# Graph network layer: blocks pick their rows in quarters of 256 edges on 32 partitions each

## The chip, the cores and the metric

The kernel runs on one core of one Trainium2 chip. The time is the device time of one execution in microseconds; it is told as the median of several runs. A profile is one more execution, recorded by the hardware profiler.

## The reference

There are N = 12500 nodes with 64 features and E = 212500 edges, sorted by their destination `dst`. An edge has a source, a destination and one weight. D = 64, H = 128.

```python
h = relu(layernorm(x))                                   # [N, 64]
edge_in = concat([h[src], h[dst], edge_weight1], axis=1)   # [E, 129]
e = silu(edge_in @ eW1 + eb1)                            # [E, 128]
e = silu(e @ eW2 + eb2)
agg = segment_sum(e, src, N)                             # [N, 128]
out = x + silu(concat([h, agg], axis=1) @ nW1 + nb1) @ nW2 + nb2
```

So rows are picked by `dst`, which is sorted, and summed by `src`, which is not.

## The kernel before

**Tables.** The first product is split by its inputs: `ta` holds h times the first 64 rows of eW1 for every node, `tb` h times the next 64. `tb0` is an early copy of the first 2048 rows of `tb`, used by blocks 0 to 29 (`EARLY`).

**Sending.** Edges are taken in blocks of 1024 (`BLK`), two blocks a pair, 104 pairs, 208 blocks. Since `dst` is sorted, 512 neighbouring edges (`HALF`) need only a short stretch of rows of `tb`. For each pair, SP loads a window `win` of four stretches of 58 rows (`WL`), which begin 25 rows (`STEP`) apart; two stretches lie on partitions 0 and up and two on partitions 64 and up (`HB`). Behind each stretch stand two constant rows, the eW1 row of the edge weight (`w1d`) and the bias (`eb1b`), put there once at the start by small POOL DMAs (L219) into three window tiles. `destinations()` works out each edge's row within its stretch and writes it to `dests`; `load_rows` broadcasts these rows to `bc`; `pick` (L368, L370) compares them with the partition's number, which gives a selecting matrix of 128 partitions by 512 columns for each block; the edges' weights go into its weight rows by a DMA (`weights`). The product `qp` (L406) multiplies `pick` and `win`: four f32 matmuls of 128 x 256 per block, each of which the trace records as two passes. ACT copies the result to `qs` (L417), adds the edge's local node number (L428), and POOL scatters 128 rows at a time (L435, eight indirect DMAs per block) into `q`, a table in DRAM that is sorted into buckets of the source node. `count` works out with DVE and two small PE products (`full`, L333 and L374) which row of its bucket each edge gets.

**Summing.** `q` is read back by batches: eleven levels of ranks times 25 groups of four buckets (`fetch`, `qt`, L486). Each of 450 steps handles four tiles of 128 edges: `lr` (L511) and `oneT` (L516) and `one` (L544) make one-hot matrices of the source, `pt` (L525, L531) adds the rows of `ta`, ACT applies silu (L535), `p` (L563) is the second product, ACT again (L567), and `seg` (L577) sums by node into `aggT` (L588). The last level is followed by the node network (`nodes`), in which `z` takes two products: L239 on 128 partitions and L242 on 64 partitions for each of two halves.

**Order.** PE, DVE, ACT and SP run their instructions in the order in which the program writes them (`manual_schedule`); POOL's order is that of the program too. The order of a step is the list `turn`, with gaps (`None`) at which pieces of `send_all` (block s is sent and block s+1 counted), of the feed (tables, checks) and of the node network are put in; a level's blocks are spread over the level before it by `marks`. Before the loop a head runs: constants, the norm of the first nodes (`x0`), `destinations()`, `sources()`, then the first tables and blocks. In the head POOL issues its DMAs and memsets one after the other:

```python
    for win in wins:
        nc.vector.memset(win, 0.0)
        for a in range(2):
            for i, row in enumerate((w1d, eb1b)):
                at = a * HB + WL + i
                for g in range(2):
                    nc.gpsimd.dma_start(win[at : at + 1, g, a, :], row[:1, :])
```

Of the kernel before, what the change touches and what calls it, by code (L numbers as in the profile page):

```python
# [28 lines left out]
F32 = mybir.dt.float32  # L29
F16 = mybir.dt.float16  # L30
BF16 = mybir.dt.bfloat16
I32 = mybir.dt.int32
# [6 lines left out]
P = 128  # L39
L = 125  # L40
WL = 58
STEP = 25
SPAN = 3 * STEP + WL
FEW = 12
HB = 64
BLK = 1024
HALF = BLK // 2
TB = BLK // P
PAIR = 2 * BLK
G = 4  # L50
# [21 lines left out]
def tile_gnn(ctx: ExitStack, tc: tile.TileContext, x, src, dst, ew, eW1, eb1, eW2, eb2, nW1, nb1, nW2, nb2, out):  # L72
# [10 lines left out]
    assert LEVELS[-1][1] == -(-E // BLK) and PAD < BLK and PAD % FEW == 0 and (-PAD) % HALF >= FEW  # L83
# [83 lines left out]
    nc.vector.tensor_scalar(plus, part, HB - 0.5, None, op0=OP.is_gt)  # L167
    nc.vector.scalar_tensor_tensor(same, plus, -float(HB), part, op0=OP.mult, op1=OP.add)
# [19 lines left out]
    dests = dram.tile([NP, 2, 2, HALF], BF16, name="dests")  # L188

    tb0 = dram.tile([P * NE, H], F32, name="tb0")  # L190
# [22 lines left out]
    for win in wins:  # L213
        nc.vector.memset(win, 0.0)
        for a in range(2):
            for i, row in enumerate((w1d, eb1b)):
                at = a * HB + WL + i
                for g in range(2):
                    nc.gpsimd.dma_start(win[at : at + 1, g, a, :], row[:1, :])  # L219
# [42 lines left out]
    with ExitStack() as work:  # L262
# [17 lines left out]
        def load_rows(s):  # L280

            if s < nblocks:
                p, g = s // 2, s % 2
                if g == 0:
                    bc = ld.tile([P, 2, HALF], BF16, name="bc")
                    lists[p] = [bc, None]
                bc, _ = lists[p]
                if g == 0 or p == 0:
                    m = 1 if p == 0 else 2
                    r = dests[p, 0, g]  # L290
                    of = bass.AP(tensor=r.tensor, offset=r.offset, ap=[[BLK, 2], [0, HB], [1, m * HALF]])
                    nc.sync.dma_start(bc[:, g : g + m].rearrange("p g e -> p (g e)"), of)
                blk[s] = [bc[:, g]]

        def load(s):

            if s < nblocks:
                p, g = s // 2, s % 2
                win = wins[p % NW]
                table, end = (tb0, NE * P) if s < EARLY else (tb, NB * P)  # L300
                assert s < EARLY or len(done_b) == NB // G
                if g == 0:
                    at = nc.sync.value_load(base_i[:, p : p + 1], min_val=0, max_val=end - SPAN)
                    for a in range(2):
                        rows = table[bass.ds(at, SPAN), :]
                        of = [[H, WL], [2 * STEP * H, 2], [1, H]]
                        of = bass.AP(tensor=rows.tensor, offset=rows.offset + a * STEP * H, ap=of)
                        nc.sync.dma_start(win[a * HB : a * HB + WL, :, a, :], of)
                    lists[p][1] = ld.tile([P, 2, HALF], F32, name="pick")
                blk[s] += [win[:, g], lists[p][1][:, g]]  # L310
            load_rows(s + 1)

        def weights(s):

            if s < nblocks:
                p, g = s // 2, s % 2
                pick = lists[p][1][:, g]
                e0 = s * BLK
                m = 1 if p == 0 or e0 + 2 * BLK > E else 2
                if m == 2 or e0 + BLK <= E:  # L320
                    of = bass.AP(tensor=ew.tensor, offset=ew.offset + e0, ap=[[HALF, 2], [BLK, m], [1, HALF]])
                    nc.sync.dma_start(lists[p][1][WL::HB, g : g + m, :], of)
                else:
                    for a in range(2):
                        m = min(HALF, E - e0 - a * HALF)
                        if m > 0:
                            of = bass.AP(tensor=ew.tensor, offset=ew.offset + e0 + a * HALF, ap=[[m, 1], [1, m]])
                            nc.sync.dma_start(pick[a * HB + WL : a * HB + WL + 1, :m], of)
# [65 lines left out]
        def send(s):  # L394
# [8 lines left out]
            two = [2 if G + t < nt else 1 for t in range(min(G, nt))]  # L403
            qps = [mm.tile([P, 2, 2, H], F32, name="qp", tag="mm") for _ in range(2)]
            for t, k in enumerate(two):
                nc.tensor.matmul(  # L406
                    qps[t // 2][:, t % 2, :k], pick[:, t * P : (t + 1) * P], win[:, :k], start=True, stop=True
                )
            parts = []
            for i, qp in enumerate(qps):  # L410
                qs = qsp.tile([P, 2, 2, W], F32, name="qs")
                mine = [(t, k) for t, k in enumerate(two) if t // 2 == i]
                same = [(slice(0, 2), 2)] if mine == [(2 * i, 2), (2 * i + 1, 2)] else [
                    (slice(t % 2, t % 2 + 1), k) for t, k in mine
                ]
                for ts, k in same:
                    nc.scalar.copy(qs[:, ts, :k, :H], qp[:, ts, :k, :])  # L417
                parts.append((i, same, qs))
            for i, same, qs in parts:
# [5 lines left out]
                places = locE[:, g * TB : (g + 1) * TB, p].rearrange("p (a i t) -> p i t a", a=2, i=2)  # L425
# [3 lines left out]
                for a in range(2):  # L429
                    for t in range(2 * i, 2 * i + 2):  # L430
                        j = a * G + t
                        if j >= nt:
# [5 lines left out]
                            in_=qs[:k, t % 2, a, :],  # L438
# [191 lines left out]
        def first_rows(g):  # L630

            hr = turned(x0, g)
            yield
            got = fp.tile([P, G, H], F32, name="got")
            product(1, hr, mm, "mm", got)
            yield
            nc.scalar.dma_start(tb0.rearrange("(p j) f -> p j f", j=NE)[:, g : g + G, :], got)
            yield
# [42 lines left out]
        def destinations():  # L681

            nc.scalar.copy(f, dstR)
            lim = lp.tile([NP, 1], F32, name="lim")
            nc.vector.tensor_scalar(lim, part[:NP], EARLY / 2 - 0.5, float((NB - NE) * P), op0=OP.is_gt, op1=OP.mult)
            nc.vector.tensor_scalar(lim, lim, float(NE * P - SPAN), None, op0=OP.add)
            yield
            nc.vector.tensor_scalar(lo[:, 0:1], fv[:, 0, 0:1], lim, None, op0=OP.min)
            for h in range(1, 4):
                nc.vector.tensor_scalar(lo[:, h : h + 1], lo[:, 0:1], float(h * STEP), None, op0=OP.add)  # L690
            for g in range(2):
                nc.vector.tensor_tensor(
                    rowsD[:, :, g, :],
                    fv[:, 2 * g : 2 * g + 2, :],
                    lo[:, 2 * g : 2 * g + 2, None].to_broadcast([NP, 2, HALF]),
                    op=OP.subtract,
                )
            nc.sync.dma_start(dests, rowsD)
            yield
            lot = mm.tile([1, NP], F32, name="lot", tag="mm")  # L700
            nc.tensor.transpose(lot, lo[:, 0:1], ident[:NP, :NP])
# [43 lines left out]
        def checks():  # L745

            ends = lp.tile([NP, 2, 4], F32, name="ends")
# [33 lines left out]
        with tc.tile_pool(name="lists", bufs=1, side="right") as lp:  # L781
# [5 lines left out]
            fv = f.rearrange("p (g e) -> p g e", e=HALF)  # L787
            lo = lp.tile([NP, 4], F32, name="lo")
            rowsD = lp.tile([NP, 2, 2, HALF], BF16, name="rowsD")
# [227 lines left out]
```

## Time and profile before

| | |
|---|---|
| median of 9 runs | 3138.19 us (3122.5 to 3166.21) |
| profiled execution: time | 3132.66 us |
| its span | 3130.4 us |
| mean granted TensorE clock | 0.875 |
| busy: PE / PE weight loads / DVE / ACT / POOL | 76 / 67 / 62 / 35 / 56% of the span |
| instructions | 45060 |
| moved by DMA | 446.69 MB, 143 GB/s in the mean |

A row of a group of instructions gives its line, engine, operation, what it writes and reads, its count, its busy time in us (overlaps counted once), the mean duration of one in ns, and the idle time of its engine just before it with what ended it. PE stands for the matmuls, PEld for the weight loads, which run beside them; SPq and POOLq are the sequencers that issue DMAs. "Clock" is the share of the full TensorE clock that the throttle granted. In a timeline a row has its start, its length, and what was run, with a count where several instructions are merged; a bracket holds the idle time before it.

### The profile page before, as it was taken

How to read it: one execution, taken by the hardware profiler on the slowest of the kernel's cores; microseconds unless marked ns; L12 is line 12 of the kernel's file. 1: busy time of each engine (PE TensorE's matmuls, PEld its weight loads, DVE VectorE, ACT ScalarE, POOL GpSimd, SP SyncE). 2: the span in 40 equal slices, each digit the busy share in tenths (PEclk: the TensorE clock that was granted, in tenths of full speed). 3: DMA queues.
4: the chain of work that ended last, by engine and by line, in shares of the span. 5: the costliest groups of instructions: out<-in, count | busy, mean ns of one | idle time of the engine just before them, and what ended most of it. 6: DMA issues, size and time to landing. Idle time of an engine off the chain costs nothing.

```text
span 3130.4 us, 45060 instructions
## 1 busy us (share of the span) xinstructions
PE 2391.0 (76%) x16009; PEld 2099.6 (67%) x16009; DVE 1955.8 (62%) x2946; ACT 1099.4 (35%) x2409; POOL 1752.6 (56%) x1739
## 2 busy tenths in 40 slices
PE   2665476566687788878887778778778888888998
PEld 1443465555577677767776667667677777788897
DVE  6665365566576666666766667666657767775443
ACT  2431222222233333333333334333334334344443
POOL 3656666666665566665665565656566666653000
PEclk9665688777788989889898899899999999999999
DMA  3543345454555555443443344334434444555441
GB/s 85 182 150 115 105 147 158 155 161 158 157 183 168 182 182 185 160 153 123 137 138 120 124 136 133 125 123 134 132 120 140 136 134 131 162 169 177 136 136 58
DMA packets 217115, 446.69 MB, mean 143 GB/s; under 512 B 41443, under 2 KB 83412, under 8 KB 216677
## 3 DMA queue, kind: packets, MB, share of 16 engines
q1 hardware_dynamic: 141897, 276.38, 27.8%
q0 software_dynamic: 54400, 123.05, 11.5%
q10 hardware_dynamic: 20586, 44.30, 4.8%
q8 instruction: 130, 2.13, 0.3%
q14 instruction: 102, 0.84, 0.1%
HBM read 257.70 MB, written 185.85 MB: 142 GB/s over the span
## 4 chain that ended last, share of the span: by engine, by line
PE 31%; DVE 10%; another core or an unknown queue 5%; issue 4%; DMA 1%; ACT 1%; POOL 1%; DVEq 0%; SPq 0%; ACTq 0%; POOLq 0%
PE p L563 7%; PE seg L577 6%; PE pt L531 6%; PE qp L406 5%; PE pt L525 3%; DVE oneT L516 2%; PE lr L511 2%; DVE one L544 1%; DVE rank L390 1%; DVE oh L340 1%; DVE mine L388 1%; DVE aggT L588 1%; POOL q L435 1%; DMA q<-qs,to 1%
## 5 line engine op out<-in xcount | busy, mean ns | idle before, releaser
L435 POOL DMA_INDIRECT q<-qs,to x1661 | 1709.7, 1029 | 1129.0 <-ACT qs L428 566.9
L535 ACT ACTIVATE e<-pt 128x512 f32<-128x512 f32 x450 | 270.2, 600 | 1110.2 <-remote 358.5
L577 PE MATMUL seg<-one,e 128*128 128x125 f32 x3600 | 528.6, 291 | 145.5 <-DVE aggT L588 82.3
L516 DVE TENSOR_SCALAR oneT<-lr,part 125x512 f32<-125x512 f32 x450 | 336.0, 747 | 447.9 <-remote 180.1
L563 PE MATMUL p<-w,e 128*128 128x128 f32 x3600 | 527.7, 289 | 93.4 <-issue 44.9
L577 PEld LDWEIGHTS seg<-one,e 128*128 128x128 f32 x3600 | 479.4, 204 | 173.5 <-issue 149.5
L563 PEld LDWEIGHTS p<-w,e 128*128 128x128 f32 x3600 | 491.0, 202 | 148.0 <-issue 59.9
L406 PEld LDWEIGHTS qp<-win,pick 128*128 128x128 f32 x1664 | 361.6, 229 | 307.0 <-issue 219.8
L531 PE MATMUL pt<-oneT,a 125*128 125x256 f32 (+1 forms) x2200 | 514.4, 361 | 44.0 <-issue 36.2
L406 PE MATMUL qp<-win,pick 128*128 128x256 f32 x1664 | 512.5, 458 | 23.0 <-issue 15.5
L417 ACT COPY qs<-qp 128x512 f32<-128x512 f32 x418 | 236.5, 585 | 586.0 <-PE qp L406 165.4
L531 PEld LDWEIGHTS pt<-oneT,a 125*128 125x128 f32 x2200 | 362.6, 204 | 81.3 <-issue 50.5
L588 DVE TENSOR_TENSOR aggT<-aggT,seg 128x500 f32<-128x500 f32 x250 | 167.7, 671 | 348.5 <-remote 111.0
L567 ACT ACTIVATE e<-p 128x512 f32<-128x512 f32 x450 | 270.6, 601 | 170.9 <-PE p L563 45.1
L525 PE MATMUL pt<-ident,qt 128*128 128x128 f32 x1800 | 298.5, 288 | 41.3 <-issue 27.8
L348 DVE TENSOR_REDUCE each<-oh 128x100 bf16<-128x800 bf16 x208 | 315.1, 1515 | 7.2
L544 DVE TENSOR_TENSOR one<-nodes,qt 128x500 f32<-128x500 f32 x450 | 302.6, 672 | 0.5 <-PE seg L577 0.5
L557 ACT COPY p<-b2f 128x512 f32<-128x512 f32 x450 | 269.0, 598 | 0.0
L525 PEld LDWEIGHTS pt<-ident,qt 128*128 128x128 f32 x1800 | 207.8, 149 | 82.4 <-issue 46.7
L388 DVE TENSOR_TENSOR mine<-oh,full 128x800 f32<-128x800 bf16 x208 | 203.9, 980 | 77.7 <-remote 35.1
L511 PE MATMUL lr<-identb,qt 128*125 128x128 bf16 x1800 | 191.2, 228 | 49.6 <-issue 30.1
L511 PEld LDWEIGHTS <-qt 128*125 128x125 bf16 x1800 | 172.4, 144 | 68.1 <-issue 56.0
(135 smaller groups left out, 1395.9 us busy)
## 6 DMA issues: line engine op xcount, KB each, us to landing
qt<-q SPq DMA_DIRECT2D x175, 576.0 KB
a<-ta SPq DMA_DIRECT2D x275, 256.0 KB
qt<-q SPq DMA_DIRECT2D x100, 288.0 KB
q<-qs,to POOLq DMA_INDIRECT x1661
bc<-dests SPq DMA_DIRECT2D x103, 256.0 KB
q<-zeros ACTq DMA_DIRECT2D x20, 1080.0 KB
q<-zeros ACTq DMA_DIRECT2D x10, 1440.0 KB
win<-tb SPq DMA_DIRECT2D x208, 58.0 KB
```

Of the source, the lines that this page charges most:

```text
L348: nc.vector.tensor_reduce(each, oh.rearrange("p t b -> p b t"), AX.X, OP.add)
L406: nc.tensor.matmul(qps[t // 2][:, t % 2, :k], pick[:, t * P : (t + 1) * P], win[:, :k], start=True, stop=True)
L435: ins = nc.gpsimd.indirect_dma_start(out=q[:], out_offset=bass.IndirectOffsetOnAxis(ap=to[:k, j : j + 1], axis=0), in_=qs[:k, t % 2, a, :] ...
L511: nc.tensor.matmul(lr[:L, t, :], loc[:, at : at + 1].to_broadcast([P, L]), identb, start=True, stop=True)
L516: nc.vector.tensor_scalar(oneT, st[k].pop("lr")[:L], part1[:L, :], None, op0=OP.is_equal)
L525: nc.tensor.matmul(pt[:, t, :], qt[:, j, :H], ident, is_transpose=True, start=t == 0, stop=False, skip_group_check=True)
L531: nc.tensor.matmul(pt[:, cols, :], a[:L, b, :], oneT[:, cols, :], start=False, stop=True, skip_group_check=True)
L535: nc.scalar.activation(e1, pt, AF.Silu)
L544: nc.vector.tensor_tensor(one.rearrange("p (b j) l -> p b j l", j=n), nodes1[:, None, None, :].to_broadcast(wide), loc[:, tiles[0][1] : ti ...
L563: nc.tensor.matmul(p2[:, t, :], e1[:, t, :], w2, start=False, stop=t == G - 1, skip_group_check=True)
L567: nc.scalar.activation(e2, p2, AF.Silu)
L577: nc.tensor.matmul(item[2][:, b, :], e2[:, t, :], one[:, t, :], start=j < G, stop=j >= G * (n - 1))
```

## The change

A block's 1024 edges are taken in four quarters of 256 edges (`QR`) instead of two halves of 512. Each quarter has a stretch of 30 rows (`WL`), 15 rows (`STEP`) from the next, eight stretches for a pair, on partitions 0, 32, 64 and 96. The constant rows stand at rows 30 and 31 of each 32 partitions, so there are 48 of the small POOL DMAs instead of 24. `bc`, `pick` and `rowsD` have 256 columns a block instead of 512. A window is loaded by four DMAs instead of two. A matmul of `qp` reads 64 partitions (two quarters), 128 columns of `pick` and up to 256 columns of `win` (a quarter's rows stand in one half of the columns and zeros in the other); the four matmuls of a block take the lower and the upper 64 partitions in turn, and the two halves write into different PSUM tiles. The start of a window is the lowest start that any of its eight quarters asks for, found with a subtraction and a minimum over `steps15`, which POOL makes with an iota; it may lie up to 16 rows (`FRONT`) ahead of the table, for which `tb0` gets 16 rows of zeros in front. The last quarter of the last pair holds only filling; its rows are moved by 20 (`far`). In the programs' order PE, ACT and POOL's scatters keep their places in the loop; SP has 208 more window DMAs with their address instructions; in the head, the iota of `steps15` is POOL's last instruction before the scatters, behind the small DMAs and the memsets of `xs`, and DVE's copy of it stands right before the memset of `srcR` (L790) and the first norm (L604).

```diff
-WL = 58
-STEP = 25
-SPAN = 3 * STEP + WL
+WL = 30
+STEP = 15
+SPAN = 7 * STEP + WL
+FRONT = 16
...
-HB = 64
+NQR = 4
...
-HALF = BLK // 2
+QR = BLK // NQR
...
-    tb0 = dram.tile([P * NE, H], F32, name="tb0")
+    tb0 = dram.tile([FRONT + P * NE, H], F32, name="tb0")
+    nc.gpsimd.dma_start(tb0[:FRONT], zeros[:FRONT, :H])
...
-        for a in range(2):
+        for a in range(NQR):
             for i, row in enumerate((w1d, eb1b)):
-                at = a * HB + WL + i
+                at = a * 32 + WL + i
                 for g in range(2):
-                    nc.gpsimd.dma_start(win[at : at + 1, g, a, :], row[:1, :])
+                    nc.gpsimd.dma_start(win[at : at + 1, g, a % 2, :], row[:1, :])
...
-                    bc = ld.tile([P, 2, HALF], BF16, name="bc")
+                    bc = ld.tile([P, 2, QR], BF16, name="bc")
...
-                    of = bass.AP(tensor=r.tensor, offset=r.offset, ap=[[BLK, 2], [0, HB], [1, m * HALF]])
+                    of = bass.AP(tensor=r.tensor, offset=r.offset, ap=[[2 * QR, NQR], [0, 32], [1, m * QR]])
...
-                    for a in range(2):
-                        rows = table[bass.ds(at, SPAN), :]
-                        of = [[H, WL], [2 * STEP * H, 2], [1, H]]
+                    for a in range(NQR):
+                        rows = table[bass.ds(at - front, SPAN), :]
+                        of = [[H, WL], [NQR * STEP * H, 2], [1, H]]
                         of = bass.AP(tensor=rows.tensor, offset=rows.offset + a * STEP * H, ap=of)
-                        nc.sync.dma_start(win[a * HB : a * HB + WL, :, a, :], of)
-                    lists[p][1] = ld.tile([P, 2, HALF], F32, name="pick")
+                        nc.sync.dma_start(win[a * 32 : a * 32 + WL, :, a % 2, :], of)
+                    lists[p][1] = ld.tile([P, 2, QR], F32, name="pick")
...
-            two = [2 if G + t < nt else 1 for t in range(min(G, nt))]
+            halves = [[sum(4 * i + 2 * a + t < nt for a in range(2)) for t in range(2)] for i in range(2)]
             qps = [mm.tile([P, 2, 2, H], F32, name="qp", tag="mm") for _ in range(2)]
-            for t, k in enumerate(two):
-                nc.tensor.matmul(
-                    qps[t // 2][:, t % 2, :k], pick[:, t * P : (t + 1) * P], win[:, :k], start=True, stop=True
-                )
+            for t in range(2):
+                for i, n_of in enumerate(halves):
+                    if n_of[t]:
+                        at = slice(64 * i, 64 * i + 64)
+                        nc.tensor.matmul(
+                            qps[i][:, t, : n_of[t]], pick[at, t * P : (t + 1) * P], win[at, : n_of[t]], start=True, stop=True
+                        )
...
             nc.scalar.copy(f, dstR)
+            far = lp.tile([NP, 1], F32, name="far")
+            for h in range(-(-LAST // QR), 2 * NQR):
+                nc.vector.tensor_scalar(far, part[:NP], NP - 1.5, float(BEYOND), op0=OP.is_gt, op1=OP.mult)
+                assert h == 2 * NQR - 1
+                nc.vector.tensor_scalar(fv[:, h, :], fv[:, h, :], far, None, op0=OP.add)
...
-            nc.vector.tensor_scalar(lo[:, 0:1], fv[:, 0, 0:1], lim, None, op0=OP.min)
-            for h in range(1, 4):
-                nc.vector.tensor_scalar(lo[:, h : h + 1], lo[:, 0:1], float(h * STEP), None, op0=OP.add)
+            base = lp.tile([NP, 1], F32, name="base")
+            nc.vector.tensor_tensor(lo, fv[:, :, 0], steps15[:NP], op=OP.subtract)
+            nc.vector.tensor_reduce(base, lo, AX.X, OP.min)
+            nc.vector.tensor_scalar(base, base, lim, low, op0=OP.min, op1=OP.max)
+            nc.vector.tensor_scalar(lo, steps15[:NP], base, None, op0=OP.add)
...
-            lo = lp.tile([NP, 4], F32, name="lo")
-            rowsD = lp.tile([NP, 2, 2, HALF], BF16, name="rowsD")
+            lo = lp.tile([NP, 2 * NQR], F32, name="lo")
+            steps15 = lp.tile([P, 2 * NQR], F32, name="steps15")
+            steps_i = lp.tile([P, 2 * NQR], I32, name="steps_i")
+            nc.gpsimd.iota(steps_i, pattern=[[STEP, 2 * NQR]], base=0, channel_multiplier=0)
+            nc.vector.tensor_copy(steps15, steps_i)
+            rowsD = lp.tile([NP, NQR, 2, QR], BF16, name="rowsD")
             nc.vector.memset(srcR[96:NP, LAST:], N)
```

## Prediction

> **What bounds the kernel now.** Profiled execution: 3132.66 us (span 3130.4); the nine runs' median, 3138.19, is 5.5 above, so differences worked out on the profile are put on the median. About 0.5% (16 us) is what a measurement of this kernel can tell from no change. I first read the page's head and a table by stage (columns: busy us of PE, PEld, DVE, ACT, POOL, then granted clock and DMA share).
>
> ```profile
> PE 2391.0 (76%) x16009; PEld 2099.6 (67%) x16009; DVE 1955.8 (62%) x2946; ACT 1099.4 (35%) x2409; POOL 1752.6 (56%) x1739
> 100.00:400.00 300.00, 169.64 (x830) 128.16 (x831) 166.70 (x247) 84.42 (x234) 189.04 (x188) 0.65 0.41 135
> 400.00:1453.00 1053.00, 774.35 (x4920) 679.11 (x4921) 672.57 (x1009) 340.05 (x747) 657.53 (x640) 0.85 0.51 163
> 1453.00:2860.00 1407.00, 1158.97 (x8084) 1037.64 (x8084) 950.30 (x1420) 535.05 (x1143) 841.40 (x813) 0.92 0.42 135
> 2860.00:3130.00 270.00, 252.87 (x2002) 228.82 (x2000) 105.56 (x173) 111.91 (x227) 23.89 (x30) 0.98 0.39 125
> ```
>
> From 400 to 2860 us the loop runs 181 blocks, 13.6 us each. PE is busy 74 to 82%, POOL 62% (with 0.30 us between its DMAs, 77% in the later part), DVE 64 to 68%. No engine is full; they wait for one another, and PE is nearest to full. After 2860 no blocks are sent. Next, the chain of waits. It reaches back to 1453 us alone; within 1453 to 2860 it is shared out so:
>
> ```profile
> by line: another core or an unknown queue 11.9%; PE p L563 11.3%; PE qp L406 10.5%; PE seg L577 10.3%; PE pt L531 9.9%; issue 8.8%; PE pt L525 4.8%; DVE oneT L516 4.4%; DVE one L544 2.9%; PE lr L511 2.9%; DVE rank L390 2.9%; DVE oh L340 2.7
> ```
>
> qp, the product that the change rewrites, is 10.5% of 1407 us, 148 us, on the path. Then the groups concerned (count, busy, mean ns, idle before):
>
> ```profile
> L406 PE MATMUL qp<-win,pick 128*128 128x256 f32 x1664 | 512.5, 458 | 23.0 <-issue 15.5 <-DMA pick<-in_edge_weight_dram 5.9 <-ACT rows_a L204 0.6
> L435 POOL DMA_INDIRECT q<-qs,to x1661 | 1709.7, 1029 | 1129.0 <-ACT qs L428 566.9 <-issue 481.5 <-ACT hr L627 13.8
> L370 DVE TENSOR_SCALAR pick<-bc,same,plus 128x1024 f32<-128x1024 bf16 x102 | 82.3, 807 | 0.0
> L368 DVE TENSOR_SCALAR pick<-bc,same,plus 128x512 f32<-128x512 bf16 x4 | 2.1, 537 | 5.9 <-DMA bc<-dests 5.9
> ```
>
> **The products.** A block now makes four f32 matmuls of 256 columns, in two passes each: eight passes on 128 partitions. After, it makes four matmuls of 256 columns again, but on 64 partitions, lower and upper half in turn, into two PSUM tiles. If the halves run side by side, eight half passes take the time of four. The trace has such a pair: L242 (64 partitions, a lower and an upper product into two PSUM tiles) between products on all 128. PE, then its weight loads:
>
> ```profile
> 2923.30 1.03 PE L531 MATMUL pt<-oneT,a 125*128 125x256 f32 x4
> 2924.17 1.01 PE L239 MATMUL z<-aggT,w1g 128*128 128x250 f32 x4
> 2925.11 0.69 PE L242 MATMUL z<-hrn,w1n 64*128 64x250 f32 x4
> 2925.74 1.16 PE L563 MATMUL p<-w,e 128*128 128x128 f32 x8
> 2926.73 0.98 PE L248 MATMUL o<-w2n,zs 128*125 128x64 f32 x8
> 2925.11 0.30 PEld L242 LDWEIGHTS z<-hrn,w1n 64*128 64x128 f32 x4 [0.32 <-issue]
> 2925.74 0.97 PEld L563 LDWEIGHTS p<-w,e 128*128 128x128 f32 x8 [0.32 <-issue]
> ```
>
> A full pass of 256 columns costs (2924.17-2923.30)/4 = 0.217 us, one of 250 columns 0.211, one of 128 columns 0.111 (eight from 1510.74 to 1511.63 in the timeline). From L239's start to L248's are 2.56 us: 4 x 0.211 for L239, 8 x 0.111 for L563, so 0.83 for L242's four half passes. One after another they would be 0.84 with nothing for switching; but the loads stood still 0.32 us at both ends (no load runs ahead there), against some 0.03 between equal passes. So the halves do overlap, 2 x 0.21 = 0.42, and going in and out costs 0.40. For qp: before 8 x 0.217 = 1.73; after 4 x 0.217 + 0.40 = 1.27; saved 0.46 us a block at full clock. At half clock a block takes 3.75 us of records (the first one, at 59.05) against 1.97 at full; I take 1.0 saved there (from nothing, if the switches grow to 1.7, to 1.7 if they cost nothing). The clock granted from 400 to 2860 is 0.89, so 22% of that time is at half: 0.78 x 0.46 + 0.22 x 1.0 = 0.58, times 181 = 105 us of PE time.
>
> [...]
>
> On the path lie 148 us of the later part's qp; its 101 blocks need 101 x (0.78 x 1.73 + 0.22 x 3.4) = 212 us, so 70%. 105 x 0.70 = 73 us is the most I expect to see; the other end is nothing. Of 73 I keep three quarters, 55: with qp shorter, PE falls to about POOL's 77%, and part of what it gains it will wait for DVE (the list of waits has PE waiting 106.9 us for DVE's each and 82.3 for aggT). The first 27 blocks I count at nothing: up to 400 us POOL's DMAs run 1.33 us apart, 188 x 1.33 = 250 of 300 us, and pace them.
>
> **Smaller parts of the loop.** The pick instruction shrinks from 1024 to 512 elements a partition: 807 to 537 ns, 0.27 x 102 = 28 us of DVE, of which the chain's share of DVE makes about 5. The broadcast bc halves from 256 to 128 KB, with DMA's share at 0.42 to 0.51: nothing, and if the load were late, a gain. The window arrives in four DMAs of 30 KB instead of two of 58: two more issues a pair at 0.40 us (two took 0.79 at 51.01). They stand in SP's queue before the next bc and later fetches of qt and a; SP spends 1250 us waiting for DVE's one before qt, which hides them (83 us of SP in all if it did not). ACT's copies and POOL's DMAs keep count and size; the second qp tile is ready earlier, the first a little later: nothing.
>
> **The head.** The constant rows of the windows go from 24 small DMAs on POOL to 48, one more DMA zeroes the front of tb0, and last in that queue, behind the memsets of xs, comes the iota of steps15. DVE's copy of it stands before srcR's memset and the first normalization, so DVE waits for all of it:
>
> ```profile
> 17.14 0.98 POOL L219 DMA_DIRECT2D win<-w1d  x2
> 27.62 0.96 POOL L219 DMA_DIRECT2D win<-eb1b  x2
> 28.57 2.11 POOL L777 MEMSET xs<- 128x768 f32 x3
> 18.00 0.47 DVE L790 MEMSET srcR<- 8x492 int32 x1
> 18.50 1.22 DVE L604 TENSOR_REDUCE mean<-x 128x16 f32<-128x1024 f32 x1
> ```
>
> 24 DMAs took 28.57-17.14 = 11.4 us. The iota ends near 30.7 + 11.4 + 0.6 (front) + 0.2 = 42.9, and DVE resumes at 43.0 instead of 18.0: 25.0 us later. Queued behind are srcR's memset (SP's load of srcR's last rows waits for it), the normalization, the destinations, and through them the first bc, the picks and POOL's first scatter (70.4). Nothing covers this. In the destinations, the far addition needs ACT's cast of f, which ended at 25.81, before the reciprocal that ran at 24.02: 1.8 more, and some four small instructions of 0.17. Head: +27.5 (25 to 30).
>
> **Sum.** 27.5 - 55 - 5 = -32: 3132.7 becomes 3100 for a profile like the one before, 3106 on the median.
>
> **Rivals.**
> - *Slower: the clock takes it back.* PE's time saved becomes idle time before the next wait, and longer stands drop the clock. Columns as in the stage table:
>
> ```profile
> 1525.00:1528.00 3.00, 0.28 (x2) 0.15 (x2) 1.32 (x2) 0.00 (x0) 2.39 (x3) 0.92 0.24 82
> 1528.00:1531.00 3.00, 2.62 (x9) 2.08 (x9) 2.93 (x5) 1.43 (x4) 0.53 (x2) 0.50 0.07 25
> 1531.00:1534.00 3.00, 2.80 (x13) 2.53 (x13) 3.00 (x4) 1.93 (x4) 2.39 (x3) 0.50 0.16 49
> ```
>
> After 3 us of idleness PE ran 6 us at clock 0.50, a loss of 3.0, or 2.1 at a path share of 0.7. If 23 blocks (one in eight) gain such a stretch, 48 of the 60 us are gone and the head decides; with 29, all: 3166. For it: clock and busy share rise together through the stages. Against: 0.58 us is short beside 3. Chance 0.17. [...]
> - *No difference: DVE is next.* PE only arrives earlier at its waits for each and aggT; a quarter of the 105 us comes through and with the 5 of pick it meets the head: 27.5 - 26 - 5, 3135. For: DVE at 68%, and those waits. Against: half of the chain is PE. 0.25.
> - *Everything on the path counts, and more at half clock:* 100 instead of 60: 3065. 0.10.
> - *The change doesn't do what it says:* the halves run in turn, eight passes stay, and 0.40 a block is added: 181 x 0.4 x 0.7 = 51, with the head 3217. Against: L242. 0.06.
>
> A window that doesn't fit would send the kernel to its slow general path; for these inputs the largest row offset within a window is 21 of the 29 allowed, the smallest 0, so it gets no chance.
>
> **How the numbers follow.** The main case has 0.42 (its own range 3085 to 3122). Faster 0.42 + 0.10 = 0.52, same 0.25, slower 0.17 + 0.06 = 0.23. The range runs from below the 3065 of the third rival, with some noise, to the 3166 of the first: 3056 to 3168.
>
> **What would show it.** qp's busy time near 400 of 512 us, its passes starting in pairs, the loads standing 0.3 us before and after; pick at 537 ns; DVE's first mean near 43 instead of 18.5 and POOL's first scatter near 98; 2860 (last scatter) earlier by 32 us. Wrong: qp's busy time unchanged (fourth rival), the clock from 400 to 2860 below 0.87 (first), or the head not moved, which would make it some 27 us faster than I say.

## The result, and the profile after

The changed kernel takes 3172.65 us in the median (3150.75 to 3194.86, 20 runs), the kernel before beside it 3135.09 us (62 runs): a ratio of 1.0123, interval 1.0103 to 1.0143, 38 us slower. The profiled execution of the change is one of its quicker ones: 3147.98 us, span 3146.2, clock 0.844 where before had 0.875.

The page's head, the stage table (columns as before) and the groups that answer to those shown of before, with `seg` and `p` of the kernel before ahead of them:

```profile
L577 PE MATMUL seg<-one,e 128*128 128x125 f32 x3600 | 528.6, 291 | 145.5 <-DVE aggT L588 82.3 <-issue 43.2 <-DVE aggT L586 8.6
L563 PE MATMUL p<-w,e 128*128 128x128 f32 x3600 | 527.7, 289 | 93.4 <-issue 44.9 <-ACT p L557 34.4 <-ACT e L535 7.9
```

```profile
PE 2339.8 (74%) x16007; PEld 1989.8 (63%) x16007; DVE 1926.5 (61%) x2953; ACT 1089.2 (35%) x2405; POOL 1755.9 (56%) x1765
...
L442 POOL DMA_INDIRECT q<-qs,to x1661 | 1700.3, 1024 | 1149.4 <-ACT qs L435 540.7
L584 PE MATMUL seg<-one,e 128*128 128x125 f32 x3600 | 544.6, 296 | 141.1 <-DVE aggT L595 68.5
L570 PE MATMUL p<-w,e 128*128 128x128 f32 x3600 | 560.3, 297 | 113.9 <-issue 73.8
L414 PE MATMUL qp<-win,pick 64*128 64x256 f32 x1662 | 323.3, 483 | 39.3 <-issue 25.0
```

```profile
100.00:400.00 300.00, 150.43 (x821) 109.67 (x822) 163.74 (x251) 87.04 (x247) 182.63 (x184) 0.58 0.40 133
400.00:1453.00 1053.00, 754.15 (x4861) 631.01 (x4860) 657.80 (x1001) 330.24 (x735) 645.74 (x637) 0.80 0.50 158
1453.00:2860.00 1407.00, 1145.71 (x8084) 988.89 (x8084) 941.03 (x1423) 533.39 (x1151) 853.58 (x824) 0.89 0.41 131
```

qp lost 189 of its 512.5 us of busy time, but PE's total fell by 51 only: the other products became longer (p 527.7 to 560.3, seg 528.6 to 544.6), with a lower clock in every stage of the loop (0.65, 0.85, 0.92 before; 0.58, 0.80, 0.89 now). The timeline of PE and its loads shows the halves side by side:

```profile
1510.46 0.21 PE L379 MATMUL full<-each,before 128*128 128x100 bf16 x1
1510.60 1.13 PE L414 MATMUL qp<-win,pick 64*128 64x256 f32 x8
1511.66 0.44 PE L518 MATMUL lr<-identb,qt 128*125 128x128 bf16 x4
...
1526.36 2.08 PE L414 MATMUL qp<-win,pick 64*128 64x256 f32 x8
1528.37 1.12 PE L532 MATMUL pt<-ident,qt 128*128 128x128 f32 x4
```

```profile
1510.35 0.10 PEld L379 LDWEIGHTS <-before 128*128 128x128 bf16 x1
1510.60 0.73 PEld L414 LDWEIGHTS qp<-win,pick 64*128 64x128 f32 x8
1511.66 0.30 PEld L518 LDWEIGHTS <-qt 128*125 128x125 bf16 x4 [0.33 <-issue]
```

From qp's start to the next product are 1.06 us at full clock and 2.01 at half; in the kernel before they are 1.79 and 3.54 (medians of the blocks without a wait). The head, POOL of before, then DVE and POOL of the change:

```profile
70.44 1.05 POOL L435 DMA_INDIRECT q<-qs,to  x1 [39.76 <-issue]
```

```profile
43.01 0.17 DVE L809 CAST steps<-steps_i 128x8 f32<-128x8 int32 x1 [24.84 <-POOL steps_i L808]
43.32 0.47 DVE L811 MEMSET srcR<- 8x492 int32 x1
43.82 1.22 DVE L611 TENSOR_REDUCE mean<-x 128x16 f32<-128x1024 f32 x1
51.16 0.35 DVE L695 TENSOR_SCALAR f<-f,far 104x256 f32<-104x256 f32 x1 [2.05 <-ACT f L690]
...
93.73 1.05 POOL L442 DMA_INDIRECT q<-qs,to  x1 [50.75 <-issue]
```

The first scatter is 23.3 us later than before, and the last begins 23.4 us later (2891.8 against 2868.4): between them, in all 208 blocks, nothing was won.

**Two kinds of chips.** The same kernel before takes quite different times on the chips that were used, so each ratio below is against runs of the kernel before on the same chip. On two chips it takes 3108 to 3146 us, as in the comparison above; on two others 2583 to 2586. The waits of ACT tell them apart, here of the kernel before on a chip of the first kind and of the second:

```profile
ACT e L535 <- remote: 358.5, 46, 19.5
ACT e L535 <- PE pt L531: 344.9, 176, 12.1
```

```profile
ACT e L535 <- PE pt L531: 607.4, 376, 6.7
ACT qs L417 <- PE qp L406: 448.5, 291, 14.9
```

"Remote" means that no instruction of this core ended where the wait ended. One such wait of the first kind, PE and then ACT:

```profile
1569.23 1.03 PE L531 MATMUL pt<-oneT,a 125*128 125x256 f32 x4
1570.09 1.05 PE L563 MATMUL p<-w,e 128*128 128x128 f32 x8
...
1571.92 1.74 PE L406 MATMUL qp<-win,pick 128*128 128x256 f32 x7
1574.23 0.38 PE L406 MATMUL qp<-win,pick 128*128 128x256 f32 x1 [0.57 <-issue]
...
1576.45 0.60 ACT L535 ACTIVATE e<-pt 128x512 f32<-128x512 f32 x1 [7.93 <-remote]
```

pt ended at 1570.26; ACT, which needs only that, starts at 1576.45, and PE meanwhile crawls along without a wait that the profile knows. Between 1567.8 and 1576.3 us the trace has one update of PE's semaphore, at 1572.11, though seven instructions that make one end in this time; then seven updates come within 0.45 us. PE's completion signals arrive late here. Where the next recorded update of PE's semaphore came more than 1 us after the end of an instruction that makes one, the stretches add up to some 1040 us in the kernel before (390 of them) and 1140 in the changed one (383), each in its first profile, on the second kind of chip to 12 and 26 us. These sums are upper bounds: the traces of the first kind also lack records (2530 updates for the 2741 instructions that make one, against 2726 on the second kind), and a missing update lengthens a stretch. What makes the signals late no trace shows. I call the two kinds late and prompt.

### The profile page after: what moved, and what is told of

The parts are those of the page before. It is cut to its first block, busy times and chain, and to the rows that moved or that the text cites. A ratio compares the mean times of both kernels' runs of the same rounds, so it can differ in the third digit from the quotient of the medians.

```text
span 3146.2 us, 45794 instructions
## 1 busy us (share of the span) xinstructions
PE 2339.8 (74%) x16007; PEld 1989.8 (63%) x16007; DVE 1926.5 (61%) x2953; ACT 1089.2 (35%) x2405; POOL 1755.9 (56%) x1765
## 5 line engine op out<-in xcount | busy, mean ns | idle before, releaser
L442 POOL DMA_INDIRECT q<-qs,to x1661 | 1700.3, 1024 | 1149.4 <-ACT qs L435 540.7
L584 PE MATMUL seg<-one,e 128*128 128x125 f32 x3600 | 544.6, 296 | 141.1 <-DVE aggT L595 68.5
L570 PE MATMUL p<-w,e 128*128 128x128 f32 x3600 | 560.3, 297 | 113.9 <-issue 73.8
L570 PEld LDWEIGHTS p<-w,e 128*128 128x128 f32 x3600 | 508.8, 208 | 195.2 <-issue 116.5
L538 PE MATMUL pt<-oneT,a 125*128 125x256 f32 (+1 forms) x2200 | 534.5, 372 | 50.0 <-issue 47.3
L538 PEld LDWEIGHTS pt<-oneT,a 125*128 125x128 f32 x2200 | 378.3, 212 | 91.0 <-issue 63.4
L424 ACT COPY qs<-qp 128x512 f32<-128x512 f32 x416 | 226.9, 589 | 527.9 <-PE qp L414 133.4
L414 PEld LDWEIGHTS qp<-win,pick 64*128 64x128 f32 x1662 | 195.0, 227 | 275.5 <-issue 217.3
L532 PE MATMUL pt<-ident,qt 128*128 128x128 f32 x1800 | 315.2, 299 | 59.1 <-issue 27.4
L414 PE MATMUL qp<-win,pick 64*128 64x256 f32 x1662 | 323.3, 483 | 39.3 <-issue 25.0
L518 PE MATMUL lr<-identb,qt 128*125 128x128 bf16 x1800 | 200.7, 235 | 60.2 <-issue 38.2
```

The source lines that it names most:

```text
L414: nc.tensor.matmul(qps[i][:, t, : n_of[t]], pick[at, t * P : (t + 1) * P], win[at, : n_of[t]], start=True, stop=True)
L442: ins = nc.gpsimd.indirect_dma_start(out=q[:], out_offset=bass.IndirectOffsetOnAxis(ap=to[:k, j : j + 1], axis=0), in_=qs[:k, t, a, :], in ...
L518: nc.tensor.matmul(lr[:L, t, :], loc[:, at : at + 1].to_broadcast([P, L]), identb, start=True, stop=True)
L532: nc.tensor.matmul(pt[:, t, :], qt[:, j, :H], ident, is_transpose=True, start=t == 0, stop=False, skip_group_check=True)
L538: nc.tensor.matmul(pt[:, cols, :], a[:L, b, :], oneT[:, cols, :], start=False, stop=True, skip_group_check=True)
L570: nc.tensor.matmul(p2[:, t, :], e1[:, t, :], w2, start=False, stop=t == G - 1, skip_group_check=True)
```

## The experiments

Times are medians in us with the kernel before on the same chip, the ratio of the two has its 95% interval, and "by 13" says that a difference is uncertain by 13 us. "Half-clock time" is the sum of the records of granted clock below 0.9 (0.5, in the first profiles of both kernels) after 400 us in the profiled run: 547 us in the kernel before, 732 in the changed one (late chips). Since these are single executions, the median clock of all runs stands beside it where it matters.

**The head alone taken back** (the changed kernel with the iota first).

```diff
+    steps_i = const.tile([P, 2 * NQR], I32, name="steps_i")      # right behind nodes1
+    nc.gpsimd.iota(steps_i, pattern=[[STEP, 2 * NQR]], base=0, channel_multiplier=0)
+    steps15 = const.tile([P, 2 * NQR], F32, name="steps15")
+    nc.vector.tensor_copy(steps15, steps_i)
...
-            steps15 = lp.tile([P, 2 * NQR], F32, name="steps15")
-            steps_i = lp.tile([P, 2 * NQR], I32, name="steps_i")
-            nc.gpsimd.iota(steps_i, pattern=[[STEP, 2 * NQR]], base=0, channel_multiplier=0)
-            nc.vector.tensor_copy(steps15, steps_i)
```

> The changed kernel, with the iota of steps15 as one of POOL's first instructions instead of behind the 48 small DMAs and the memsets; nothing else moves. If the head's 23 us (first scatter at 93.7 us instead of 70.4) pass to the end whole, the time falls by 20 to 25 us to about 3150, and the loop alone is then some 13 us slower than before. If the early blocks, which wait for POOL, absorb the head, it stays near 3172.

On a prompt chip it takes 2554.66 against 2582.69, a ratio of 0.9890 (0.9876 to 0.9905).

> e1 once more, beside e5. If the kernel before takes some 2583 us: 2555 as before. If it takes some 3135, as in the first comparison: the head's 23 us come off the changed kernel's 3172, 3149, still 0.4% above the kernel before.

On a late chip it takes 3150.88 against 3141.86, a ratio of 1.0025 (0.9992 to 1.0059). The head explains most of the 38 us, and the loop, which was to win 60, wins nothing there.

**The halves alone** (the kernel before, eight half products of 128 columns).

```diff
+            halves = [min(G, max(0, nt - a * G)) for a in range(2)]
+            qps = [mm.tile([P, G, H], F32, name="qp", tag="mm") for _ in range(2)]
+            for t in range(G):
+                for a in range(2):
...
+                        at = slice(64 * a, 64 * a + 64)
+                        nc.tensor.matmul(
+                            qps[a][:, t], pick[at, t * P : (t + 1) * P], win[at, a], start=True, stop=True
```

> The kernel before (58 rows, halves of 512 edges, same head, same DMAs), with the products alone changed: each half of the partitions multiplies its own stretch, eight matmuls of 128 columns in turn between the halves, into one PSUM tile for each half. Theory A (the clock takes the gain back): qp's busy time falls from 512 to some 330 us, the granted clock falls from 0.875 to about 0.85, the other PE lines get longer by 60 to 100 us in sum, and the time stays at 3135 within 15. Theory C (the halves gained their 55 us, and the rest of the change in the loop lost them: more issues on SP, smaller DMAs, the first result later): 3080, with the clock near 0.87.

On a prompt chip: 2578.26 against 2582.69, 0.9986 (0.9974 to 0.9998).

> The kernel before, with qp alone made in halves: eight matmuls of 64 partitions x 128 columns a block, the lower and the upper half in turn; pick, bc, windows and head stay as before. Where the chain's waits are marked remote and the kernel before takes near 3140: theory A (PE's gain is handed back: PE is slowed by its own late signals and by more time at half clock) expects 0.996 to 1.004 and a clock of 0.85 to 0.86 instead of 0.875; theory B (the time on the path counts, and the quarters' other parts cost the 55 us) expects 0.98 to 0.985. Where the kernel before takes near 2585: 0.997 to 1.0 by both, since POOL's scatters set the pace there.

On a late chip: 3150.44 against 3146.42, 1.0022 (0.9998 to 1.0045), with 688 us of half-clock time. Over all runs the median clock is 0.842, against 0.866 for the kernel before on this chip. The groups of PE in this late run:

```profile
L576 PE MATMUL seg<-one,e 128*128 128x125 f32 x3600 | 558.4, 298 | 126.8 <-issue 72.0
L562 PE MATMUL p<-w,e 128*128 128x128 f32 x3600 | 557.9, 298 | 99.6 <-issue 66.1
...
L409 PE MATMUL qp<-win,pick 64*128 64x128 f32 x3322 | 334.0, 332 | 59.7 <-issue 47.7
```

qp is 178 us of busy time shorter than in the first profile of before, as in the change; seg and p are 30 us each longer, and the time is not shorter.

**The quarters without the halves** (qp on 128 partitions, windows four quarters wide, zeros elsewhere; eight full passes a block).

```diff
-    wins = [const.tile([P, 2, 2, H], F32, name=f"win{i}") for i in range(NW)]
+    wins = [const.tile([P, 2, NQR, H], F32, name=f"win{i}") for i in range(NW)]
...
+                for b in range(0, fulls[t], 2):
+                    e = min(b + 2, fulls[t])
+                    nc.tensor.matmul(qps[t][:, b:e], pick[:, t * P : (t + 1) * P], win[:, b:e], start=True, stop=True)
```

> The changed kernel with all of its quarters, windows, DMAs and head, but the products on all 128 partitions: the four quarters' rows stand in 512 columns, four matmuls of 256 columns a block on 128 partitions, eight whole passes as before. Theory A: only the head is left, 3160 within 12, clock back at 0.87, qp's busy time back at 510. Theory C: the loop's losses without the gain, 3210 or more.

On a prompt chip: 2583.16 against 2582.69, 1.0002 (0.9992 to 1.0013).

> The changed kernel with qp on all 128 partitions (windows four quarters wide, zeros outside a quarter's own columns; eight full passes of 256 columns as before): quarters, pick and head of the change without the halves side by side. Near 3140 for the kernel before: theory A expects the head alone, 1.005 to 1.009, with the clock back at 0.87 to 0.88; theory B expects the head and the quarters' other cost, 1.02 to 1.03. Near 2585: 0.999 to 1.001 by both.

On a late chip: 3190.53 against 3146.42, 1.0147 (1.0104 to 1.0190), between what the two theories expected: with the head at 23 to 29 us, some 17 to 23 (by 14) are left for the quarters. The clock, 0.864 in the median against 0.866, is back near that of before, though below the 0.87 to 0.88 expected.

**What PE's time is worth.** First the products of the changed kernel made twice, then those of the kernel before:

```diff
-            for t in range(2):
+            for t in (0, 1, 0, 1):
```

```diff
-            for t, k in enumerate(two):
+            for t, k in [*enumerate(two)] * 2:
```

> The changed kernel with each half product made twice into the same place: 0.87 us more PE work a block at full clock, the same two switches. Theory A: PE is kept busier, the clock rises to about 0.86, and the time stays within 15 of the changed kernel's 3172. If PE time in the loop is worth 0.7 of itself, as the prediction had it: 208 blocks x 0.95 x 0.7 = 140 us more, about 3310; with three quarters of that, 3275.

On a prompt chip: 2591.39 against 2582.69, 1.0029 (1.0017 to 1.0041). The changed kernel itself is at 0.9989 on the other prompt chip (below), so 199 us more busy time of qp (281.5 to 480.7) cost some 10 us (by 4).

> The kernel before with each of the four qp matmuls of a block made twice, 181 x 1.73 = 313 us more PE work at full clock from 400 to 2860 us, and 2.0 us a block more of half-clock time where it applies. Near 3140: theory A expects at most 60 us (1.02), with a clock of 0.91 or more; theory B, at the 0.7 of the path that the prediction used, 220 us or more (1.07). Near 2585, where POOL sets the pace: under 40 us (1.015), unless PE becomes full, which its busy share then shows.

On a late chip: 3195.59 against 3146.42, 1.0129 (1.0076 to 1.0182), with a clock of 0.91 in the median against 0.866, and 416 us of half-clock time in the profiled run.

```profile
L406 PE MATMUL qp<-win,pick 128*128 128x256 f32 x3328 | 875.3, 419 | 50.5 <-issue 36.6
...
L577 PE MATMUL seg<-one,e 128*128 128x125 f32 x3600 | 511.2, 286 | 97.5 <-DVE aggT L588 38.6
...
L563 PE MATMUL p<-w,e 128*128 128x128 f32 x3600 | 512.5, 284 | 66.7 <-issue 36.7
```

363 us more of qp cost 0.0129 x 3146 = 41 us, 0.11 a us (0.07 to 0.16). The other products got shorter as the clock rose. This is the run that prices the term on which the prediction rested; it prices time added, and the two runs with time taken away stand beside it below.

**The pick twice** (the changed kernel with the iota first, the pick instruction repeated), some 55 us more of DVE.

> e1 with DVE's pick comparison of 512 elements a partition made twice (0.54 us more DVE work a pair, 55 us in all, the second of the same result). Theory D (where the kernel before takes some 2583 us, POOL's scatters run without a pause, and the loop gains only what makes a scatter shorter: those beside the old 1024-element pick were long in 69% of cases, those beside the 512-element one in 4%): two short instructions don't lengthen scatters as one long one did, so the time stays at 2555 within 6, and DVE's time alone is worth nothing. Theory E (DVE's time in the loop is what the loop gained: 28 us saved on pick, some 25 gained): 50 us given back, 2605.

On a late chip: 3149.81, 1.0028 (0.9996 to 1.0060), against 1.0025 without the second pick on the same chip, 1 us more (by 15): DVE's time is worth nothing that these runs can tell. On a prompt chip it was not run.

**Change and kernel before again**, each unedited, on a prompt chip.

> The changed kernel unchanged. The kernel before took 2583 us beside the first four experiments, against 3135 in the first comparison, so the effect must be measured again under these conditions. If the kernel before is again near 2583: e1 was 28 us faster than before and the head is 23 us, so about 2578, no difference from before (theory A' : the loop gains some 28 us, the head takes 23 of them back). If the kernel before is near 3135: 3172 as in the first comparison.

> The kernel before, for a profile under the same conditions. If it takes 2583 us: the waits that end by 'remote' (358.5 us before ACT's silu of pt, 180.1 before oneT) and the 'issue' stands of PE's loads are gone, the loop is paced by POOL's scatters and the waits for them, and the granted clock is near 0.94. If it takes 3135: as in the first profile.

The change takes 2580.81 against 2585.9, 0.9989 (0.9978 to 1.0); the kernel before, once more, took 2585.45. On a prompt chip the change is not slower at all. The chain of waits there by line (whole span, before, then changed), and POOL's group in both:

```profile
DMA q<-qs,to 19%; POOL q L435 15%; PE seg L577 5%; PE pt L531 5%; PE qp L406 5%; PE p L563 5%; DVE each L348 3%; PE pt L525 3%; DVE oneT L516 3%; DVE mine L388 2%; DVE rank L390 2%; DVE one L544 2%; DVE oh L340 2%; DVE aggT L588 2%; DMA qt<-q 2%
...
L435 POOL DMA_INDIRECT q<-qs,to x1661 | 1733.9, 1044 | 558.8 <-issue 452.5
```

```profile
DMA q<-qs,to 22%; POOL q L442 19%; PE seg L584 5%; PE pt L538 4%; PE p L570 4%; PE pt L532 2%; DVE mine L393 2%; PE qp L414 2%; DVE oneT L523 2%; DVE one L551 2%; DVE rank L395 2%; DVE each L353 2%; DVE oh L345 2%; DVE aggT L595 1%; PE lr L518 1%
...
L442 POOL DMA_INDIRECT q<-qs,to x1661 | 1717.6, 1034 | 560.8 <-issue 444.4
```

POOL scatters nearly without a pause (between the first and the last scatter of before only four gaps are over 0.5 us, 15 us together): it is the pace, and PE's time hides behind it. From the first scatter to the end of the last the changed kernel needs 24 us less: 16.3 because a scatter takes 1034 instead of 1044 ns, and 8 because the four long gaps add up to 6.8 instead of 14.8 us. The shorter scatters go with the pick. POOL and DVE, before, then changed:

```profile
958.15 1.26 POOL L435 DMA_INDIRECT q<-qs,to  x1 [0.30 <-issue]
...
958.49 0.80 DVE L370 TENSOR_SCALAR pick<-bc,same,plus 128x1024 f32<-128x1024 bf16 x1
```

```profile
950.96 0.97 POOL L442 DMA_INDIRECT q<-qs,to  x1 [0.30 <-DMA q<-qs,to]
...
951.11 0.54 DVE L375 TENSOR_SCALAR pick<-bc,same,plus 128x512 f32<-128x512 bf16 x1
```

Of the scatters beside a pick of 1024 elements 67 to 72% last over 1.07 us, of those beside one of 512 elements 4 to 7%; the mean falls from 1158 to 983 ns for some 107 scatters, 19 us, and that of all others stays (1036 and 1038). Why scatters are long beside the long pick and seldom beside the short one, which is the same kind of operation, no run here shows.

**The change taken apart on one late chip**, all four beside the same 29 runs of the kernel before (3107.97 us).

> The changed kernel without halves and without the late head: quarters, the narrow pick and the small windows alone (qp on all 128 partitions, the iota of steps15 at the start). Where the kernel before takes near 3140: if PE's time has slack and the quarters cost nothing (theory A), 0.998 to 1.003; if the quarters' loop costs what is left of the 46 us of the quarters with the late head (theory C), 1.006 to 1.010. Where it takes near 2585: 0.988 to 0.992, since POOL's scatters are shorter beside the narrow pick.

> The changed kernel with the iota at the start. Near 3140 for the kernel before: 1.000 to 1.006, as before; less e7_quarters_alone this gives the halves, which theory A puts at 0 (-10 to +10 us) and the prediction's sum at -55 us. Near 2585: 0.987 to 0.991, and 0 to 6 us below e7_quarters_alone.

> The changed kernel itself, beside the others: above e1_third by the head alone, 22 to 29 us, in every condition.

> The changed kernel with its qp matmuls made twice, 181 x 0.87 = 157 us more PE work at full clock in the loop. Near 3140: theory A, with the price of 41 us for 313 that doubling qp in the kernel before showed, expects 10 to 30 us above after_third and a clock of 0.86 to 0.88; by the path share of the prediction it would be 110 us. Near 2585: 5 to 15 us above after_third, as before.

| kernel | median, us | ratio | half-clock time, us |
|---|---|---|---|
| quarters alone (no halves, iota first) | 3129.5 | 1.0063 (1.0032 to 1.0094) | 589 |
| and halves (the change with the iota first) | 3102.05 | 0.9960 (0.9933 to 0.9988) | 694 |
| and the late head (the change) | 3129.48 | 1.0070 (1.0032 to 1.0107) | 729 |
| and its products twice | 3180.19 | 1.0207 (1.0169 to 1.0244) | 609 |

From row to row, by the ratios: quarters +20 us, halves -32 (0.0103 x 3108, uncertain by 13), head +34 (by 15), products twice +43 (by 17) for 228 us more busy time of qp (331.8 to 559.9), 0.19 a us. So theory C holds for the quarters, which do cost something in the loop. The halves win part of what was forecast, which theory A did not expect. On the other late chip the same step is some -11 us (by 17; 8 us with the halves, 46 less a head of 27 without), and alone they won nothing. The products twice cost more than the 10 to 30 us expected.

**SP's window loads.** Four DMAs of 29 rows instead of two of 58 in the kernel before, beside the quarters alone and the kernel before. They were meant to find the quarters' 20 us, but ran on a prompt chip, where the quarters win.

```diff
-                    for a in range(2):
+                    for a, b in ((0, 0), (0, WL // 2), (1, 0), (1, WL // 2)):
...
-                        nc.sync.dma_start(win[a * HB : a * HB + WL, :, a, :], of)
+                        nc.sync.dma_start(win[a * HB + b : a * HB + b + WL // 2, :, a, :], of)
```

> The kernel before with each window loaded by four DMAs of 29 rows instead of two of 58: 208 more DMAs on SP, nothing else. Near 3110 to 3140 for the kernel before: if the quarters' cost in the loop is SP's DMAs (theory D), 1.004 to 1.008 (12 to 25 us of the 83 us that they hold SP's queue); if they are hidden behind SP's wait for DVE's one, as the prediction had it, 0.998 to 1.002. Near 2585: 0.999 to 1.001 by the prediction, since POOL sets the pace.

> The quarters alone once more, beside e8_four_loads. Near 3110 to 3140: 1.003 to 1.009; theory D expects it within 8 us of e8_four_loads, and the prediction's zero term that it stands 15 us or more above it. Near 2585: 0.988 to 0.992.

> The kernel before, for a trace on the same chip: 1.00. In the loop SP's wait for DVE's one before a batch's load is 1000 us or more, and shorter by the window DMAs' time in the two others.

Four loads take 2598.7 against 2585.05: 1.0055 (1.0041 to 1.0069), 14 us and not the nothing expected; the quarters alone take 2559.53, 0.9907 (0.9893 to 0.9921); the kernel before 2581.8, 0.9991 (0.9977 to 1.0005). SP's queue and its longest wait, the kernel before and the one with four loads:

```profile
1614.45 0.77 SPq L308 DMA_DIRECT2D win<-tb  x2
SPq L486 <- DVE one L544: 1344.8, 259, 11.4
```

```profile
1605.15 4.61 SPq L308 DMA_DIRECT2D win<-tb  x4
SPq L486 <- DVE one L544: 966.3, 234, 10.3
```

The 404 loads after 100 us hold SP 475 us here, against 85 us for the 202 of the kernel before, far more than the double; the quarters' own loads of 30 rows take 173 us beside them. SP's wait for DVE's one gave up 379 us (and 105 with the quarters alone, to 1239.5), so it hid nearly all of the 390 us, as the prediction had it. If the 14 us are SP's, the quarters' 88 us would cost some 3 by the same price, an estimate for prompt chips; on a late one it was not run. But a load of 29 rows is not a quarter's load of 30 in other respects too. The trace has 2 updates of the semaphore that tells of completion for nearly each load of 29 rows, 3 for one of 58 and up to 16 for one of 30, and the last of them comes 6.35, 4.93 and 2.99 us after the issue (medians). So the 14 us may be windows that land later, and this run doesn't test the number of issues alone.

## Why the prediction was wrong

| step | forecast | late chips | prompt chips |
|---|---|---|---|
| head | +27.5 | +34 (by 15) | +26 (by 5) |
| halves: PE's time on the path | -55 | -32 (by 13) in the quarters, +7 (-1 to 14) alone | -4 |
| smaller parts of the loop | -5 | +20 (10 to 29) | -24 (-20 to -28) |
| sum | -32 | +22 (10 to 33), and +38 (32 to 45) in the comparison of record | -3 (-6 to 0) |

The prompt column takes the head as 0.9989 - 0.9890 from two chips, and its halves are those alone.

**The head held.** DVE's first mean came at 43.82 (43 forecast), the wait of 2.05 us for ACT's cast as told, and the delay reaches the end about one to one (23.3 us at the first scatter, 23.4 at the last; 34, by 15, and 26, by 5, of the time). The first scatter came 4 us earlier than forecast (93.73 against 98), since on the way there the 2048-element operation that makes t took 1.22 us instead of 3.21, and the second pick waited 3.39 us for its bc instead of 5.93. Right by mechanism and size.

**The overlap held and was undersized.** 1.06 us at full clock instead of the forecast 1.27, 2.01 at half instead of 2.75: the loads stood still 0.33 us behind qp as forecast, but only 0.15 ahead of it. The forecast's 1.73 and 3.75 us for a block before are 1.79 and 3.54 when they are taken like these, from start to start (3.75 is the length of the records). By the prediction's own formula the freed PE time is then (0.78 x 0.73 + 0.22 x 1.53) x 181 = 164 us instead of 105. Before over after, a block's products are 1.79 / 1.06, 1.7 times as fast.

**The step that failed is "105 x 0.70 = 73, of 73 I keep three quarters, 55".** It took a share of the chain of waits as the price of PE's time. The price measured on late chips is 0.11 (qp twice in the kernel before) and 0.19 (in the changed one) for a us of qp's busy time added; for a us taken away it is nothing with the halves alone (7 us slower with 178 less) and 0.17 in the quarters (32 us for 188). None is near the 0.5 to 0.7 of the prediction. Two things take the rest. First, PE hands time back through the clock: with less to do, its half-clock time grows (547 to 688 with the halves alone, 589 to 694 in the quarters, 547 to 732 in the change) and shrinks with more (416 and 609), so the change's 185 us more, at a recorded clock of 0.5, lose some 92 us of full-clock work by my estimate, half of what qp gave. The medians of the clock over all runs on one chip say the same (0.866 to 0.842 with the halves alone and to 0.91 with qp twice; 0.865 to 0.841 with the halves in the quarters), while the quarters without halves leave it nearly alone (0.864 and 0.865, against 0.866 and 0.869). This is the first rival's mechanism, and its mark came too: the clock from 400 to 2860 us is (1053 x 0.80 + 1407 x 0.89) / 2460 = 0.85, below 0.87. But its price was wrong as well, since that lost PE work is worth as little as the rest. Second, on late chips the loop waits for PE's signals rather than for PE: up to 1040 us of the profiled execution of the kernel before and 1140 of the changed one's lie in stretches in which a finished product is not yet known to be finished, and a shorter product in front of such a stretch would end in the same wait. That this is where the time goes is argued from the waits; no run could take the late signals away. The hint stood in the lines shown: "another core or an unknown queue 11.9%" was the largest share of the chain, above qp, and the prediction gave it no cost.

**"DVE is next" did not hold by its mechanism:** 55 us more of DVE changed nothing that could be measured (1 us, by 15, on a late chip). Its size, a quarter of PE's freed time, was nearer to what was measured than the main case's. **"The halves run in turn" did not hold:** qp's busy time (323.3 us against 512.5) and its start times (the eight half passes of a block in 1.06 us at full clock) rule it out.

**The smaller parts were mis-signed, in both directions.** On prompt chips the quarters alone win 24 us, most of it, by the traces, through the short pick (the 19 us above), and not for DVE's sake but for POOL's, whose scatters it stretches less; the prediction counted the pick for DVE alone. No run changed the pick by itself there. On late chips POOL waits for ACT's qs anyway (540.7 us), and the quarters cost 20 us, on two chips alike (there 46 less the head's 27). Where these 20 us come from stays open: a second pick cost nothing there, SP's loads were priced on a prompt chip only, and no trace of the kernel before was taken on the chip of the four runs. The kernels without halves also have wider windows and another order of rows in qs than the change, so a part of the 20, and of the halves' 32, may belong to these.

## What to carry to other kernels

A share of the chain of waits says where time passes in one execution, not what shortening that work is worth: double the work and measure (here 0.11 to 0.19 us a us, where the chain said 0.7). Where the chain names an unknown queue as its largest part, be slow to price any engine's share in full. A small constant made last in a busy POOL queue here delayed what stood in order behind its reader (DVE's first mean from 18.50 to 43.82 us, the first scatter by 23.3, the last by 23.4); made first it left the mean at 18.58, and the change with the iota first is 1.1% faster than the kernel before on prompt chips, and 0.4% faster or 0.25% slower, the latter within the noise, on late ones.

## What the hardware showed beside

- The same kernel takes some 2585 us on two chips and 3108 to 3146 on two others, with the granted clock at 0.94 or 0.87; on the late kind PE's completions reach the other engines late, by 2.7 us in the mean of the 390 stretches of the kernel before (an upper bound, as said).
- In the first profiles of the kernel before and of the change, half clock came in stretches that are multiples of 3.41 us, the last of each trace aside. Cut into windows of that length, the kernel before (late) has 87 such stretches after 100 us. In the window ahead of each PE was busy for at most 2.24 us, in 69 of them for less than 1.55; up to the last of these stretches 491 windows were followed by full clock, and all had 1.55 or more. The last window of each half-clock stretch had 2.89 us or more. So a partly busy window went ahead of half clock, and a saving of 0.73 us a block (1.79 to 1.06), short beside 3, went with more of it: 547 us in the kernel before, 732 in the changed one.
- On a prompt chip the window loads of 29 rows held SP for 1.17 us in the mean: those that begin at partitions 0 and 29 for 0.30 and 0.65, those at 64 and 93, which are issued third and fourth, for 1.83 and 1.92. The quarters' loads of 30 rows held it for 0.43 in the mean, whatever their partition (0.40 to 0.45).
